# First cross-attention of a four-layer Flamingo stack: key weights folded into the query weights, value weights into the output weights

## The chip, the cores and the metric

The kernel runs on one core of one Trainium2 chip, in fp32. Its metric is the device time of one execution in microseconds (us). TensorE is written PE, VectorE DVE, ScalarE ACT, GpSimd POOL, and SyncE, which issues most loads, SP.

## The reference

Four layers, each a cross-attention and then a mixture of experts (or of LoRA adapters). x and the context are 16 batches of 128 tokens by 256 features. The change touches the attention of layer 0 only. It has 16 heads of 16 features, and each of the three projections is one 16x16 matrix that all heads share:

```python
kh = einsum('nshd,ed->nshe', k.reshape(N, S, 16, 16), Wk)     # k = ctx
qh = einsum('nshd,ed->nshe', q.reshape(N, S, 16, 16), Wq)     # q = layernorm(x)
vh = einsum('nshd,ed->nshe', v.reshape(N, S, 16, 16), Wv)     # v = ctx
attn = softmax(einsum('nqhd,nkhd->nhqk', qh, kh) / sqrt(16))
out = einsum('nhqk,nkhd->nqhd', attn, vh).reshape(N, S, 256) @ Wo.T
x = x + tanh(g_xattn[0]) * out
x = x + tanh(g_ffn[0]) * experts_0(layernorm(x))              # top 2 of 8, gelu
```

There is no bias in this attention, so energy = q Wq' Wk k' and out = attn v Wv' Wo' with block-diagonal matrices, and the products Wq' Wk and Wv' Wo' don't depend on the data.

## The kernel before

The 16 batches are handled in 4 blocks of 4 batches (512 tokens). A block is normalized (ln_block: statistics with bnst L250, xn on ACT L321, transposes ps_ln L344, xnT on ACT L348), projected to queries (ps_q L975) and keys (ps_k L975, copied to kT by ACT L1201). The queries are written twice, masked to even and odd heads (qM, one half by ACT L1225 and one by DVE L1220), so that one matmul of 32 rows serves two heads. Each batch then has its values projected (ps_v L987) and spread by an ACT copy (L1250) into one of three zeroed tiles in which each head has its own columns; its scores (ps_s L1259), exps (e, ACT L1274), values and denominators (ps_o L1315, 64 small matmuls), the reciprocal of the denominators (rs, DVE L1326), the product oT (DVE L1328), the output (ps_y L1337) and the addition to x (DVE L363). Each rs is also added to a running sum by POOL (sum_range L1126); rs has two buffers, so the reciprocal of batch b waits until POOL has added that of batch b-2.

Beside the attention runs what the experts need. POOL fills the sorted token buffer xg with zeros by 15 DMAs (L2416, function clear), from a tile made of a piece of kT. When a block of x is done, the router (front of Moe: ps_logitsT L426, ps_router L434, small DVE operations L377 to L553) finds the place of each token, and POOL scatters its rows into xg by 8 indirect DMAs (L558). After two blocks a plan of expert slots is made (DVE L637 to L722, its integers plan_i L712), SP reads it into registers and loads each slot's tokens (xr) and weights (w), and the first 12 slots of layer 0 (ps_h L1659, hT L1664, ps_e L866) are worked off, at first beside the rest of the routing.

The order of PE, ACT and DVE is written out by the kernel: the parts above are generators, a planner (class Clock) estimates from cost formulas when each part could start, and the part that is due is emitted. So a change in any part can change the whole order of the three engines. SP and POOL get their order from the framework's scheduler. DMAs of one queue are issued in its order.

```python
att = Fast16(0, pool, keys_in(pool), w, ctxT, watch)
attend([(att, clear, behind)], early(), eager=True, express=2)
```

Of the kernel before, what the change touches and what calls it, by code (L numbers as in the profile page):

```python
# [8 lines left out]
F32 = mybir.dt.float32  # L9
# [10 lines left out]
P = 128  # L20
B = 16
S = 128
D = 256
KC = D // P
NBLK = 4
BPB = B // NBLK
TB = BPB * S
H16, DH16 = 16, 16
# [62 lines left out]
def kernel(ctx: ExitStack, tc: tile.TileContext, a: dict, out: bass.AP):  # L91
    nc = tc.nc
# [6 lines left out]
    class Ring:  # L99


        def __init__(self, pool):
            self.pool, self.made = pool, []
# [8 lines left out]
    ps_x = Ring(ctx.enter_context(tc.tile_pool(name="ps_x", bufs=4, space=PSUM)))  # L112
# [6 lines left out]
    def load_x(bs):  # L119
# [7 lines left out]
    ident = const.tile([P, P], F32, tag="ident", name="ident")  # L127
# [3 lines left out]
        out=gates, in_=a["rows"][:, slice(*_ROWS["gates"])].to_broadcast([P, 8])  # L131
# [4 lines left out]
    def col(name, i):  # L136
        lo = _COLS[name][0] + i
        return cols[:, lo:lo + 1]

    def row(name):  # L140
        lo, hi = _ROWS[name]
        return rows[:, lo:hi]
# [14 lines left out]
    for e in range(NE):  # L157
# [9 lines left out]
        out=tri, in_=ones, compare_op=ALU.is_gt, fill=0.0, base=0,  # L167
# [27 lines left out]
    def tgx(i):  # L195
        return tg[:, i:i + 1]

    def gate_down(pool, i):

        gate = pool.tile([P, 1], F32, tag=f"gate{i}", name="gate", bufs=1)  # L200
        nc.vector.tensor_scalar(gate, tgx(i), DOWN, None, ALU.mult)
        return gate
# [780 lines left out]
    def project_values(layer, ps, w, src, tok):  # L983

        if layer == 0:
            for c in range(KC):
                nc.tensor.matmul(  # L987
                    ps[:, c * P:(c + 1) * P], lhsT=src[:, c, tok], rhs=w[:, 0, :],
                    start=True, stop=True,
                )  # L990
            return
        for k in range(KC):
            nc.tensor.matmul(
                ps, lhsT=src[:, k, tok], rhs=w[:, k, :], start=(k == 0), stop=(k == KC - 1)
            )
# [121 lines left out]
    class Watch:  # L1117
# [10 lines left out]
        def fine(self, good, behind):  # L1128
# [9 lines left out]
            nc.vector.tensor_reduce(good, eq, AX.X, ALU.add)  # L1138
            return self.n * P

    def keys_in(pool):
        return lambda: pool.tile([P, KC, TB], F32, tag="kT", name="kT", bufs=2)

    class Fast16:
# [3 lines left out]
        def __init__(  # L1148
            self, layer, pool, kpool, w, ctxT, watch, mask=None, bias=None, others=None
        ):  # L1150

            self.others = others
            self.bias = bias
            self.gate = tgx(1) if layer == 1 else gate_down(pool, layer)
            self.layer, self.pool, self.kpool = layer, pool, kpool
            self.ctxT, self.watch, self.mask = ctxT, watch, mask
            self.w = w

            self.qb = pool.tile([P, KC, 2], F32, tag=f"qb{layer}", name="qb", bufs=1)
            if layer == 0:  # L1160
                nc.vector.memset(self.qb, 0.0)
            else:
                for c in range(KC):
                    nc.vector.tensor_scalar(
                        self.qb[:, c, :], mask2, col(f"l{layer}_bq", c), None, ALU.mult
                    )

            self.vs = []
            for i in range(3):
                v = pool.tile([P, H16, 2 * DH16], F32, tag=f"v{layer}{i}", name="v", bufs=1)  # L1170
                nc.gpsimd.memset(v, 0.0)
                self.vs.append(v)
            self.qM, self.kT, self.es, self.os = {}, {}, {}, {}

        def prepare(self, blk, before):


            made = [self.queries(blk, before)]
            if blk not in self.kT:
                made.append(self.keys(blk))  # L1180
            if self.others is not None:

                if blk == 0:
                    made.append(self.keys(1))
                for later in (0, 1, 2) if blk == 0 else (3,) if blk == 1 else ():
                    made.append(self.others.keys(later))
            return made
# [43 lines left out]
        def scores(self, b, tick):  # L1231
            layer, pool = self.layer, self.pool
            wv = self.w[2]
            blk, tok = b // BPB, slice(b % BPB * S, (b % BPB + 1) * S)
            pv = ps_x.tile([P, H16, DH16], F32, tag="x", name="ps_v")
            project_values(layer, pv.rearrange("p h d -> p (h d)"), wv, self.ctxT[blk], tok)
            if layer == 1:
                v = pool.tile([P, H16, DH16], F32, tag="vb", name="vb", bufs=3)
            else:
                v = self.spread(self.vs[b % 3])  # L1240
                pv = pv.rearrange("p (j e) d -> p j e d", e=2)
            if layer:
                bv = row(f"l{layer}_bv")
                nc.vector.tensor_tensor(
                    v, pv,
                    bv.rearrange("p (h d) -> p h d", d=DH16) if layer == 1
                    else bv.rearrange("p (j e d) -> p j e d", e=2, d=DH16), ALU.add,
                )
            else:
                nc.scalar.copy(v, pv)  # L1250

            tick()


            pss = [ps_mm.tile([P, 4, S], F32, tag="mm", name="ps_s") for _ in range(4)]
            for c in range(KC):
                for j in range(4):
                    part = slice(j * 32, (j + 1) * 32)
                    nc.tensor.matmul(  # L1259
                        pss[j][:, 2 * c:2 * c + 2, :], lhsT=self.kT[blk][part, c, tok],  # L1260
                        rhs=self.qM[blk][part, c, :, tok], start=True, stop=True,
                    )
                if c == 0:
                    tick(False)
            es = []
            for j in range(4):
                e = pool.tile([P, 4, S], F32, tag="e", name="e", bufs=9)
                if layer == 2:
                    nc.scalar.activation(
                        e, pss[j], AF.Exp, bias=self.mask[0][:, b:b + 1],  # L1270
                        scale=self.mask[1][:, b:b + 1],
                    )
                else:
                    nc.scalar.activation(e, pss[j], AF.Exp)  # L1274
                es.append(e)
            self.es[b] = es
            if layer == 1:

                both = pool.tile([P, 2, H16], F32, tag="sums", name="sums")
                sums, rs = both[:, 0], both[:, 1]  # L1280
                by_pair = sums.rearrange("p (c j e) -> p j c e", c=KC, e=2)
                for j, e in enumerate(es):
                    nc.vector.tensor_reduce(
                        by_pair[:, j], e.rearrange("p (c e) s -> p c e s", e=2), AX.X, ALU.add
                    )
                nc.vector.reciprocal(rs, sums)
                self.watch.see(both.rearrange("p i h -> p (i h)"))
                nc.vector.tensor_tensor(
                    self.spread(self.vs[b % 3]), v.rearrange("p (j e) d -> p j e d", e=2),
                    rs.rearrange("p (j e) -> p j e", e=2)[:, :, :, None].to_broadcast(  # L1290
                        [P, H16 // 2, 2, DH16]
                    ), ALU.mult,
                )
            tick(False)
# [987 lines left out]
    watch = Watch(KC * S, "a")  # L2282
# [46 lines left out]
    def layers(fast):  # L2329
# [40 lines left out]
        with tc.tile_pool(name="context", bufs=1) as cpool, ExitStack() as for_mid:  # L2370
            ctxT = []
# [15 lines left out]
            with tc.tile_pool(name="att0", bufs=2) as pool:  # L2387
                w = attention_weights(0, pool)
# [57 lines left out]
                def early():  # L2446
                    while not started:
                        yield 1
                    yield from started[0]
# [5 lines left out]
                    lanes = []  # L2455
                behind, plans = routed(moe, turns, start)
                if fast:
                    att = Fast16(0, pool, keys_in(pool), w, ctxT, watch)
                    attend([(att, clear, behind)], early(), eager=True, express=2)
                else:  # L2460
                    general(shifted(pool, 0, w, ctxT), None, behind)
# [5 lines left out]
            with for_slots, tc.tile_pool(name="lanes0", bufs=2) as pool:  # L2467
                lanes = lanes + lane0(pool, LANES - len(lanes))
                job = slots0(moe, NSLOT - n, plans[-1:], lanes, tiles(fpool, bufs0))
                for i, _ in enumerate(job):  # L2470
                    if i == 24:
                        ws = [attention_weights(layer, wpool) for layer in (1, 2)]
                        if not biases:

                            t = stat.tile([P, BPB, ROW], F32, tag="xn", name="bias_rows", bufs=3)
                            nc.sync.dma_start(
                                out=t[:, 0, 0:D],
                                in_=a["l2_b2"][NE:NE + 1].to_broadcast([P, D]),
# [24 lines left out]
            with tc.tile_pool(name="mid", bufs=2) as pool:  # L2503
                lora = Lora(pool, wpool, biases["base_b"])
                if fast:
                    att = Fast16(
                        2, pool, lambda: shared_tile(spool, "kT"), ws[1], ctxT, watch, mask,
                        biases["l2_bo"],
                    )
# [29 lines left out]
        with ExitStack() as for_last:  # L2539
            with tc.tile_pool(name="ffn2", bufs=2) as pool:  # L2540
# [11 lines left out]
                if fast:  # L2552
                    wpool = right(for_last, "weights3")
                    att = Fast3(wpool, watch)
# [38 lines left out]
    ps = ps_x.tile([1, len(watches)], F32, tag="x", name="ps_good")  # L2593
# [9 lines left out]
    with tc.If(again > 0):  # L2603
        load_x(range(B))
        layers(fast=False)
# [90 lines left out]
```

## Time and profile before

| | |
|---|---|
| median of 8 runs | 1589.59 us (1586.75 to 1593.02) |
| profiled execution, its own time | 1587.12 us |
| span of its profile | 1585.4 us |
| mean granted PE clock | 0.977 |
| first attention with its routing | 0 to about 133 us |
| first 12 slots of experts | from 134.5 us |
| HBM read, written | 272.88 MB, 48.18 MB |

The span is the time between the first and the last instruction of the profile. Times inside the profile are counted from the start of the span. A line number L followed by digits is a line of the kernel before; in the changed kernel the lines behind the edits stand 21 to 42 further down (ps_s L1301, ps_o L1357, rs L1368, oT L1370, ps_y L1379, the v copy L1288, the zero fills L2458).

### The profile page before, as it was taken

The numbers are of one execution on the slowest core, as the hardware profiler recorded it, in microseconds if no ns is written. First come the engines' busy times: TensorE is split into PE (matmuls) and PEld (weight loads), VectorE is DVE, ScalarE is ACT, GpSimd is POOL, SyncE is SP. The second block draws the span as 40 slices with busy tenths as digits, with TensorE's granted clock in tenths as the row PEclk, the third lists the DMA queues.
The fourth block names the chain that finished last, engine by engine and source line by source line (L and its number), as shares of the span: only waits on it lengthen the run. The fifth ranks groups of instructions, "written<-read, shape, count | busy, mean of one in ns | idle before, by whom it ended". The sixth has DMA issues, their size and how long they took to land.

```text
span 1585.4 us, 34879 instructions
## 1 busy us (share of the span) xinstructions
PE 1483.1 (94%) x12752; PEld 1171.9 (74%) x12752; DVE 864.6 (55%) x2763; ACT 649.0 (41%) x1550; POOL 369.0 (23%) x485
## 2 busy tenths in 40 slices
PE   6897899999999999899999999999999999997992
PEld 4676889999656567655559999999955656677892
DVE  3685312222279767766346555556743627477655
ACT  5566323335556566652125333334453334224110
POOL 4242411111532212434000110111150002023531
PEclk9899999999999999999999999999999999999996
DMA  9914683534420000111064412411351000033956
GB/s 322 384 41 152 193 267 99 198 98 148 98 40 1 2 6 23 43 41 54 0 238 148 154 48 99 165 32 32 105 109 19 14 1 29 2 102 124 312 171 215
DMA packets 109368, 171.52 MB, mean 108 GB/s; under 512 B 17273, under 2 KB 79294, under 8 KB 109184
## 3 DMA queue, kind: packets, MB, share of 16 engines
q1 hardware_dynamic: 85344, 114.22, 22.6%
q0 software_dynamic: 20304, 49.66, 10.0%
q10 hardware_dynamic: 3536, 5.25, 1.0%
q8 instruction: 108, 1.77, 0.4%
q14 instruction: 76, 0.62, 0.1%
HBM read 272.88 MB, written 48.18 MB: 203 GB/s over the span
## 4 chain that ended last, share of the span: by engine, by line
PE 79%; DVE 10%; DMA 5%; ACT 3%; issue 2%; POOL 0%; SPq 0%; DVEq 0%; ACTq 0%; POOLq 0%
PE ps_w L1836 16%; PE ps_e L866 12%; PE ps_h L1659 7%; PE ps_w L1773 7%; PE ps_qk L2096 5%; PE ps_v L2205 3%; PE ps_o L1315 3%; PE ps_s L2226 2%; PE ps_q L978 2%; PE ps_g L1884 2%; PE ps_y L2274 2%; PE ps_y L1337 2%; PE ps_s L1794 2%; PE ps_s L1259 2%; PE ps_k L978 2%
## 5 line engine op out<-in xcount | busy, mean ns | idle before, releaser
L1836 PEld LDWEIGHTS ps_w<-xT,w 128*128 128x128 f32 x2304 | 264.3, 192 | 2.5 <-issue 0.2
L1836 PE MATMUL ps_w<-xT,w 128*128 128x128 f32 x2304 | 265.1, 275 | 0.0
L878 POOL DMA_INDIRECT yd<-y,to x117 | 118.6, 1014 | 569.9 <-DVE c L841 305.8
L866 PE MATMUL ps_e<-w,hT 128*128 128x256 f32 x848 | 197.8, 380 | 2.5 <-DVE hT L1743 1.9
L866 PEld LDWEIGHTS ps_e<-w,hT 128*128 128x128 f32 x848 | 154.8, 190 | 21.4 <-DVE hT L1743 2.8
L1844 ACT ACTIVATE u<-ps_w,b 128x128 f32<-128x128 f32 x312 | 89.5, 367 | 175.4 <-PE ps_w L1836 170.3
L1659 PE MATMUL ps_h<-xT,w 128*128 128x128 f32 x1120 | 137.4, 283 | 13.8 <-DMA w<-in_l_w_dram 7.0
L1659 PEld LDWEIGHTS ps_h<-xT,w 128*128 128x128 f32 x1120 | 135.7, 199 | 16.8 <-issue 8.6
L1847 DVE SCALAR_TENSOR_TENSOR m<-ps_w,b,u 128x128 f32<-128x128 f32 x312 | 87.6, 344 | 109.0 <-PE ps_w L1836 94.8
L1664 ACT ACTIVATE hT<-ps_h,b 128x128 f32<-128x128 f32 x312 | 88.6, 373 | 129.4 <-issue 82.5
L558 POOL DMA_INDIRECT xg<-xn,xi x96 | 93.7, 976 | 99.2 <-issue 53.0
L1773 PE MATMUL ps_w<-xnT,sw 128*128 128x512 f32 x256 | 111.9, 594 | 0.0
L874 DVE SCALAR_TENSOR_TENSOR y<-ps_e,c,bias 128x256 f32<-128x256 f32 x78 | 37.6, 483 | 135.1 <-PE ps_e L866 134.3
L1126 POOL TENSOR_TENSOR sum_range<-sum_range,rs 128x256 f32<-128x256 f32 x48 | 35.3, 736 | 247.5 <-DVE rs L2253 137.7
L1773 PEld LDWEIGHTS ps_w<-xnT,sw 128*128 128x128 f32 x256 | 48.3, 190 | 56.7 <-issue 50.9
L831 DVE COPY xT<-ps_xr 128x256 f32<-128x256 f32 x117 | 48.6, 418 | 75.4 <-PE ps_xr L829 75.4
L1326 DVE RECIPROCAL rs<-ps_o 128x256 f32<-128x256 f32 x32 | 56.1, 1754 | 32.9 <-PE ps_o L1315 22.9
L1274 ACT ACTIVATE e<-ps_s 128x512 f32<-128x512 f32 x128 | 65.9, 602 | 18.5 <-PE ps_s L1259 18.5
L321 ACT ACTIVATE xn<-x,nmr,rstd 128x256 f32<-128x256 f32 x128 | 67.8, 596 | 12.4 <-DVE nmr L314 9.1
L2232 ACT ACTIVATE e<-ps_s 128x512 f32<-128x512 f32 x64 | 33.5, 601 | 74.3 <-PE ps_s L2226 74.2
L1315 PE MATMUL ps_o<-e,v 128*32 128x128 f32 x1536 | 53.5, 282 | 9.2 <-DVE x L363 3.9
L858 ACT ACTIVATE bias<-b,c 128x256 f32<-128x256 f32 x78 | 40.5, 519 | 51.6 <-DVE c L844 20.8
(272 smaller groups left out, 2550.5 us busy)
## 6 DMA issues: line engine op xcount, KB each, us to landing
w<-in_l_w_dram SPq DMA_DIRECT2D x160, 1024.0 KB
w<-in_l_w_dram SPq DMA_DIRECT2D x39, 512.0 KB
kT<-in_l_wgu_dram SPq DMA_DIRECT2D x39, 512.0 KB
xg<-zeros POOLq DMA_DIRECT2D x15, 1170.0 KB, 25.3
b<-in_l_b_dram SPq DMA_DIRECT2D x80, 128.0 KB
xr<-xg SPq DMA_DIRECT2D x78, 130.0 KB
kT<-in_l_w_dram SPq DMA_DIRECT2D x39, 256.0 KB
x<-yd POOLq DMA_DIRECT2D x48, 128.0 KB, 4.6
```

What stands on the lines that cost most here:

```text
L321: nc.scalar.activation(xns[:, i, 0:D], src, AF.Identity, bias=nmr[:, i:i + 1], scale=rstd[:, i:i + 1])
L558: self.unordered(nc.gpsimd.indirect_dma_start(out=xg[:, :], in_=xns[:, i, :], in_offset=None, out_offset=bass.IndirectOffsetOnAxis(ap=xi[: ...
L866: nc.tensor.matmul(po, lhsT=hT[:, f, :], rhs=lane(s)["w2"][:, f, :], start=(f == 0), stop=(f == nf - 1),)
L878: self.unordered(nc.gpsimd.indirect_dma_start(out=yd[:, :], in_=y, in_offset=None, out_offset=bass.IndirectOffsetOnAxis(ap=to[:, 0:1], axi ...
L1315: nc.tensor.matmul(po[32 * j:32 * (j + 1), i, c, :], lhsT=w if i else v[:, c * HPC + 2 * j + e, :], rhs=es[j][:, 2 * c + e, :], start=(e = ...
L1659: nc.tensor.matmul(ps[:, i, :], lhsT=w["w1"][:, k, f * P:(f + 1) * P], rhs=xT[:, k, :], start=(k == 0), stop=(k == KC - 1),)
L1664: nc.scalar.activation(hT[:, f, :], ps[:, i, :], AF.Gelu, bias=w["b1"][:, f:f + 1])
L1773: nc.tensor.matmul(ps, lhsT=wt[:, k, f * P:(f + 1) * P], rhs=xnT[:, k, :], start=(k == 0), stop=(k == KC - 1),)
L1836: nc.tensor.matmul(ps[:, f, :], lhsT=wt[:, k, s, f * P:(f + 1) * P], rhs=xT[:, k, :], start=(k == 0), stop=(k == KC - 1),)
L1844: nc.scalar.activation(u[:, f, :], pair[0][:, f, :], AF.Identity, bias=w["b1"][:, i:i + 1])
L1847: nc.vector.scalar_tensor_tensor(m1[:, f, :], pair[1][:, f, :], w["b3"][:, i:i + 1], u[:, f, :], ALU.add, ALU.mult,)
L2096: nc.tensor.matmul(ps, lhsT=w[:, k, c * P:(c + 1) * P], rhs=src[:, k, :], start=(k == 0), stop=(k == KC - 1),)
```

## The change

At the start PE turns Wq, Wk and Wv (each laid out as a 128x128 block-diagonal of its 16x16 matrix), and makes two products from them: Wq' Wk, which takes the place of Wq, and Wv' Wo', which takes the place of Wo. Then the keys are the context itself, which is already in SBUF transposed (ctxT), and the values are the context itself in rows. Projections of keys and values with their copies are gone. The rows of the context are loaded by SP, 512 KB for each block, that of block blk+1 when block blk is prepared; the tile has two buffers. ACT spreads them where it spread the projected values. The zeros for xg are made from ctxT instead of kT. Since the planner sees other parts, it writes another order for the three engines up to the first slots.

```diff
+    def folded(pool, w):
+        wq, wk, wv, wo = w
+        ps = ps_x.tile([P, 3, P], F32, tag="x", name="ps_turned")
+        for i, v in enumerate((wq, wk, wv)):
+            nc.tensor.transpose(ps[:, i, :], v[:, 0, :], ident)
+        t = pool.tile([P, 3, P], F32, tag="turned", name="w_turned", bufs=1)
+        nc.vector.tensor_copy(t, ps)
+        ps = ps_x.tile([P, P], F32, tag="x", name="ps_qk0")
+        nc.tensor.matmul(ps, lhsT=t[:, 0, :], rhs=t[:, 1, :], start=True, stop=True)
+        both = pool.tile([P, 1, P], F32, tag="wqk", name="w_qk", bufs=1)
+        nc.vector.tensor_copy(both[:, 0, :], ps)
+        ps = ps_x.tile([P, KC, D], F32, tag="x", name="ps_vo0")
+        for c in range(KC):
+            nc.tensor.matmul(
+                ps[:, c, :], lhsT=t[:, 2, :], rhs=wo[:, c, :], start=True, stop=True
+            )
+        out = pool.tile([P, KC, D], F32, tag="wvo", name="w_vo", bufs=1)
+        nc.vector.tensor_copy(out, ps)
+        return [both, None, None, out]
...
+            self.rows = {}
+            if layer == 0:
+                self.kT = dict(enumerate(ctxT))
+                self.load_rows(0)
+
+        def load_rows(self, blk):
+            t = self.pool.tile([P, BPB, D], F32, tag="crows", name="ctx_rows")
+            nc.sync.dma_start(
+                out=t,
+                in_=a["ctx"][blk * TB:(blk + 1) * TB, :].rearrange("(b p) d -> p b d", p=P),
+            )
+            self.rows[blk] = t
...
         def prepare(self, blk, before):
+            if self.layer == 0 and blk + 1 < NBLK:
+                self.load_rows(blk + 1)
             made = [self.queries(blk, before)]
             if blk not in self.kT:
                 made.append(self.keys(blk))
...
-            pv = ps_x.tile([P, H16, DH16], F32, tag="x", name="ps_v")
-            project_values(layer, pv.rearrange("p h d -> p (h d)"), wv, self.ctxT[blk], tok)
+            if layer:
+                pv = ps_x.tile([P, H16, DH16], F32, tag="x", name="ps_v")
+                project_values(
+                    layer, pv.rearrange("p h d -> p (h d)"), wv, self.ctxT[blk], tok
+                )
...
-                nc.scalar.copy(v, pv)
+                nc.scalar.copy(
+                    v, self.rows[blk][:, b % BPB, :].rearrange(
+                        "p (j e d) -> p j e d", e=2, d=DH16
+                    )
+                )
...
-                    att = Fast16(0, pool, keys_in(pool), w, ctxT, watch)
+                    att = Fast16(0, pool, None, folded(pool, w), ctxT, watch)
```

More of the change, by code (lines that the diff above doesn't have):

```diff
@@ L1240, in scores @@
                 v = self.spread(self.vs[b % 3])
-                pv = pv.rearrange("p (j e) d -> p j e d", e=2)
             if layer:
@@ L1244, in scores @@
                 nc.vector.tensor_tensor(
-                    v, pv,
+                    v, pv if layer == 1 else pv.rearrange("p (j e) d -> p j e d", e=2),
                     bv.rearrange("p (h d) -> p h d", d=DH16) if layer == 1
```

## The prediction

> **What bounds the kernel now.** I read the page's engine totals first, then the stage table over the first attention, then the waits of VectorE (DVE) and GpSimd (POOL), the chain of waits, and POOL's timeline. The totals say TensorE (PE); the stage table corrects that for the only stretch that the change touches.
>
> ```profile
> PE 1483.1 (94%) x12752; PEld 1171.9 (74%) x12752; DVE 864.6 (55%) x2763; ACT 649.0 (41%) x1550; POOL 369.0 (23%) x485
> ```
> ```profile
> 0.00:50.00 50.00, 35.64 (x400) 22.15 (x400) 17.82 (x49) 27.79 (x54) 21.88 (x71) 0.93 0.96 336
> 50.00:100.00 50.00, 47.10 (x674) 34.72 (x678) 38.98 (x111) 32.11 (x72) 12.97 (x17) 0.90 0.65 244
> 100.00:133.00 33.00, 27.00 (x493) 20.65 (x482) 30.16 (x88) 15.63 (x35) 14.15 (x20) 1.00 0.17 56
> 133.00:240.00 107.00, 92.99 (x607) 86.79 (x608) 32.24 (x163) 45.51 (x122) 25.42 (x28) 0.94 0.67 216
> ```
> Columns: stretch, length, busy us of PE, weight loads, DVE, ACT, POOL, then PE clock, DMA share, GB/s. PE is full only in 50 to 100 us (47.1 of 50). Before that it idles 14.4 us while the DMA engines are saturated (0.96); after it DVE is the full engine (30.2 of 33); from 133 to 240 PE idles 14 us at the start of the expert slots, and later it is full to the end. So PE work that goes pays at face value in one stage of three.
>
> What ends the first stage is a queue on POOL:
>
> ```profile
> DVE rs L1326 <- POOL sum_range L1126: 7.4, 1, 7.4
> POOL xg L2416 <- DMA xg<-zeros: 16.5, 6, 3.5
> ```
> ```profile
> 23.05 22.97 DMA xg<-zeros
> ...
> 46.92 0.88 POOL sum_range L1126
> ...
> 47.82 1.77 DVE rs L1326
> ```
> The first pair reads: waiting engine and line, releaser, total us, times, longest. POOL issues fifteen zero fills of 1170 KB; nine go out at once and each of the last six waits for a landing. Behind them stands POOL's first sum_range, which frees the two-buffer tile rs. So the third reciprocal (batch 2) waits 7.4 us on DVE until 47.82. That is gate 1. Gate 2 is of the same kind:
>
> ```profile
> 89.70 1.11 POOL L558 DMA_INDIRECT xg<-xn,xi  x1 [5.23 <-ACT xn L321]
> ...
> 98.71 0.96 POOL L558 DMA_INDIRECT xg<-xn,xi  x1 [0.30 <-issue]
> 99.70 0.74 POOL L1126 TENSOR_TENSOR sum_range<-sum_range,rs 128x256 f32<-128x256 f32 x1
> ```
> The eight scatters of a routed block hold POOL for about 10 us (89.70 to 99.67) ahead of a sum_range; the reciprocal of batch 10 follows at 100.63.
>
> **What goes and comes.** Key projection: 16 matmuls, 10.62 us of PE, and eight kT copies, 4.68 us of ACT. Value projection: 64 matmuls, 11.29 us of PE. Together 21.9 us of PE; by stage 11.7 before 50 us, 7.6 in 50 to 100, 2.6 in 100 to 133. Fold: three transposes (0.29 us, row of ps_ln), one 128x128 product (0.30, row of ps_v) and two of 256 columns (0.41, row of ps_y) make 2.0 us; by the cold ps_k rows at the start (1.1 us against 0.6 later) up to 3.7. It lies where PE has 3.75 us of work (now removed) before 14.95 us; if that cover failed, 2 to 4 us would fall on the first block, ahead of gate 1, which swallows them. Its three DVE copies, about 1.3 us, stand ahead of the first LayerNorm's small operations, in DVE's 3.06 us wait for ACT: nothing.
>
> The sixteen v copies stay on ACT, now reading SBUF. No row shows this copy; ACT's copy from PSUM is 375 ns on average (347 the shortest), its 128x256 operation from SBUF, xn, 596 ns. So 0 to +3.5 us of ACT in all; a saving can't be excluded (265 ns for the half-size logitsT gives -1.8). I take +1.5: the shape is that of the first, the memory that of the second, and 4.7 us of kT copies go besides. ACT is never full here (15.6 of 33, 32.1 of 50), and the 1.15 us of ps_s hide a copy. Once v was late by more than that, each exp behind it on ACT would be late by the rest.
>
> [...]
>
> **What moves, and this decides.** (1) The context comes a second time, as rows: four loads of 512 KB. The first two go out on SP's queue behind the last x loads, at about 20.2 and 20.7 us by the rows of the loads issued there now; that is after POOL's first nine fills. The 1.05 MB go through saturated engines (387 GB/s in a typical slice of that stretch): 2.7 us. A third load wants its buffer when block 0's values are copied; some 0.8 us more of it fall ahead of the last fill. Bounds: 0 (rows served behind the fills) to 4.1 (a third load in full). I take +3.5, so the reciprocal of batch 2 starts at 51.3 for 47.82. The first v copy (25.85 now) waits for its rows until some 30 to 33 us, because a 128 KB load of that queue took 0.9 to 1.5 us; ACT's exp of batch 0 (26.11 now) is queued behind it, and PE behind that. Gate 1 covers this: three batches at about 4 us of PE fit before 51.
>
> (2) The planner writes another order. DVE's two masked query writes of block 1 (1.52 us) stand ahead of the reciprocal of batch 2 now (at 37.86), and behind it and its oT after the change. So the scores of batch 4 wait for gate, reciprocal 1.77, oT 0.43 and qM 0.8 to 1.5: about 54.5, against 52.83. Block 3's qM likewise goes behind the reciprocal of batch 10, which gate 2 holds.
>
> (3) Between 51 and 90 PE does 7.6 us less, and this wins back some of the 3.5. But DVE has 39 us of work in that stage plus the moved 1.5 and becomes the full engine; the block's routing needs its last x through the same DVE. My walk along the new orders with the durations above gives, now and after: reciprocal of batch 7 at 81.8 and 83.5, of batch 8 at 88.7 and 90.5; scatter from 89.7 and about 90.5; batch 10, behind the scatter, 100.6 and 101.6; batch 12, 114.6 and 115.2. Here the loss is almost regained.
>
> (4) The second block's scatter moves. Now it stands ahead of the sums of batches 12 and 13 and ends at 123.7. After, its positions are written just ahead of the reciprocal of batch 13 (121.6), and the sum of batch 13 is behind it: 121.6 + 8 x 1.26 + 0.8 = 132.5. The reciprocal of batch 15 waits for that buffer: 132.8, against 128.7 now. The last x add starts a reciprocal (1.77), an oT (0.43) and an output (1.3, from 130.89 to 132.17) later: 136.3 for 132.17.
>
> (5) The plan's integers (plan_i L712, 122.72 now, 9 us ahead of the last x) come behind the last x and small operations of the routing on DVE, at about 139.3. SP's plan reads and weight loads follow them; now it takes SP 11.7 us from the plan to the issue of slot 1's first weights (122.96 to 134.66) and some 5 us to land. Two loads of the next attention's weights are placed ahead of the plan read on SP, and wait for the last work of this attention, so they add little. Slot 1's first products start at 156 to 158 instead of 143.50. Against that, front work that PE does there now (two LayerNorm transposes, the router: 2.6 us) and slot 0's second half are done in the wait. Slot 1's second half starts at 166.8 to 168.8, against 160.60: +6 to +8. The later weight stall (4.3 us at 183.6) shrinks by 0 to 2, as the scatters no longer share the queue. From 240 us the PE order is the same in both kernels and PE is full, so what is left arrives at the end: +4 to +8, and I take +5, in the lower half because the walk adds every wait at full length.
>
> [...]
>
> **The sum.** The profiled execution took 1587.12 us (span 1585.4, 1.7 around it), 2.5 below the median 1589.59. With +5: 1592.1 for such an execution, 1594.5 for the median.
>
> **Rivals.** *A gain.* If the rows are served behind the fills, gate 1 stays at 47.8; the 7.6 us of PE in 50 to 100 then count for about 5 (DVE binds for the rest), the last x comes at 127 to 129, and the plan's later place costs nothing that PE hasn't won: 1582 to 1586. For it: PE's 47.1 of 50; against it: both gates and the full DVE of 100 to 133. *Nothing.* Gate 1 at +2, some 4 us won, and slot 1 late by 2 to 4: 1588 to 1592. *A larger loss.* One mechanism, at SP: the next layer's weight loads ahead of the plan read hold it until the last exp and sum_range, and the 11.7 us chain starts after that; slot 1's second half slips by 10 to 13 us: 1599 to 1603. It decides as soon as the read is later than 142 us. *The fold does not do what it says*: the products and copies named above are gone from the changed order, so I give this nothing.
>
> **The numbers.** What a measurement of this kernel can tell from no change is about 0.2%, 3.2 us. Forecast (1592.5 to 1598) 0.50; gain 0.15; nothing 0.18; larger loss 0.17. Of the forecast 0.05 lies within 3.2 us: faster 0.15, same 0.23, slower 0.62. The range 1585.5 to 1602 leaves out most of the gain (0.12) and the end of the loss (0.07).
>
> **What would show it.** Right: the first sum_range at 50 to 51 instead of 46.92; a DVE wait on POOL at batches 2, 10 and 15; the last x add at 135 to 139; slot 1's first products past 154; then an equal shift to the end. Wrong: a first sum_range by 48, or a last x add before 132, which would mean that PE's saving got through; or a shift that goes away again between 170 and 240 us in weight stalls that the slots have anyway.

## The result, and the profile after

On chips where the kernel before takes 1589 us the changed kernel is slower: median 1602.15 us (16 runs) against 1589.12 (45 runs of the kernel before), ratio 1.0081, 95% interval 1.0071 to 1.0092, about +13 us. The forecast had the side and the places right and the size too small (+5): the median lies 0.15 us above the upper end of its range (1602). A later comparison on another chip, where the kernel before takes 1664 us, gave 0.9979 (0.9964 to 0.9993) for the same pair; the last section returns to it. Everything up to there is from chips of the first kind unless it says otherwise.

The profiled execution of the changed kernel took 1600.13 us (span 1598.3). Engine totals, then the stage table with the columns of the prediction (stretch, length, busy us of PE, weight loads, DVE, ACT, POOL, PE clock, DMA share, GB/s):

```profile
PE 1479.3 (93%) x12681; PEld 1168.6 (73%) x12681; DVE 864.7 (54%) x2766; ACT 639.9 (40%) x1538; POOL 369.0 (23%) x485
```
```profile
0.00:50.00 50.00, 29.05 (x297) 18.92 (x297) 16.93 (x47) 22.48 (x44) 19.57 (x69) 0.86 0.96 334
50.00:100.00 50.00, 43.60 (x727) 31.61 (x727) 40.88 (x112) 32.48 (x74) 14.37 (x20) 0.93 0.76 285
100.00:133.00 33.00, 26.26 (x441) 20.42 (x441) 24.28 (x68) 15.72 (x35) 11.33 (x14) 0.84 0.10 34
133.00:240.00 107.00, 88.21 (x549) 79.90 (x550) 35.90 (x173) 37.47 (x107) 28.27 (x33) 0.87 0.65 207
```
PE is busier in no stage than before, and its granted clock is lower in three of the four: 0.86 for 0.93 before 50 us, 0.84 for 1.00 in 100 to 133, 0.87 for 0.94 behind it. The profile's windows show where: the clock is 0.50 from 52 to 58 us, from 104 to 108 and from 138 to 156. PE is called cold there, and warm where the clock is 1.00. DVE, 91% busy in 100 to 133 before, now waits there too (24.3 of 33). The waits of DVE and POOL name the gates (waiter, releaser, total us, times, longest):

```profile
DVE rs L1368 <- POOL sum_range L1126: 13.9, 3, 6.6
```
```profile
POOL xg L2458 <- DMA xg<-zeros: 19.0, 7, 4.6
```
Three reciprocals wait for POOL instead of one: batch 2 (6.60 us), batch 10 (4.42) and batch 15 (2.90). How PE comes out of the first of these is seen in its timeline (start, length, line, what, and in brackets the idle time before it with its releaser):

```profile
53.10 2.09 PE L1301 MATMUL ps_s<-qM,ctxT 32*128 32x256 f32 x16 [5.32 <-DVE qM L1256]
55.12 1.94 PE L1357 MATMUL ps_o<-e,v 128*32 128x128 f32 x32
...
59.54 1.15 PE L1301 MATMUL ps_s<-qM,ctxT 32*128 32x256 f32 x16
60.61 1.08 PE L1357 MATMUL ps_o<-e,v 128*32 128x128 f32 x32
```
The scores wait 5.32 us for block 1's qM, and then the same sixteen matmuls take 2.09 us that take 1.15 a batch later. The last of the three waits, batch 15, stands behind the second block's scatter and one sum (POOL, then DVE):

```profile
133.47 0.96 POOL L558 DMA_INDIRECT xg<-xn,xi  x1 [0.30 <-issue]
134.46 0.73 POOL L1126 TENSOR_TENSOR sum_range<-sum_range,rs 128x256 f32<-128x256 f32 x1
```
```profile
135.22 1.76 DVE L1368 RECIPROCAL rs<-ps_o 128x256 f32<-128x256 f32 x1 [2.90 <-POOL sum_range L1126]
```
The end of the attention and the start of the slots, on DVE and on PE:

```profile
139.67 0.48 DVE L363 SCALAR_TENSOR_TENSOR x<-ps_y,gate,x 128x256 f32<-128x256 f32 x1
...
141.19 0.18 DVE L712 CAST plan_i<-plan 128x36 int32<-128x36 f32 x1
```
```profile
137.58 2.05 PE L1379 MATMUL ps_y<-w_vo,oT 128*128 128x256 f32 x4 [5.16 <-DVE oT L1370]
...
147.91 3.42 PE L418 MATMUL ps_router<-wgl,xnT 128*128 128x8 f32 x16
...
152.40 6.10 PE L1701 MATMUL ps_h<-xT,w 128*128 128x128 f32 x32 [0.55 <-DVE xT L831]
...
159.24 3.84 PE L1701 MATMUL ps_h<-xT,w 128*128 128x128 f32 x32 [0.30 <-DVE xT L831]
...
169.62 5.47 PE L1701 MATMUL ps_h<-xT,w 128*128 128x128 f32 x32 [2.47 <-DMA w<-in_l_w_dram]
```
The last x add is 7.5 us late (132.17 before), the plan 18.5. Behind them PE works cold: router 3.42 us (1.85 before), slot 0's first products 6.10 (3.84 when warm), and PE waits 2.47 us for slot 2's weights. The kernel before has a cold place here too, one slot later: slot 1's first products take 6.62 us behind a wait of 4.73.

### The profile page after: what moved, and what is told of

Same layout as the page of the kernel before. It is cut to its first block, busy times and chain, and to the rows that moved or that the text cites. A ratio compares the mean times of both kernels' runs of the same rounds, so it can differ in the third digit from the quotient of the medians.

```text
span 1598.3 us, 34723 instructions
## 1 busy us (share of the span) xinstructions
PE 1479.3 (93%) x12681; PEld 1168.6 (73%) x12681; DVE 864.7 (54%) x2766; ACT 639.9 (40%) x1538; POOL 369.0 (23%) x485
## 4 chain that ended last, share of the span: by engine, by line
## 5 line engine op out<-in xcount | busy, mean ns | idle before, releaser
L1368 DVE RECIPROCAL rs<-ps_o 128x256 f32<-128x256 f32 x32 | 56.2, 1756 | 43.6 <-PE ps_o L1357 26.7
```

The lines of the kernel that those rows point to most:

```text
L1368: nc.vector.reciprocal(rs, po[:, 1])
```

## Experiments

The first four ran on one chip with the kernel before at 1591.14 us. The changed kernel was not run beside them; its loss is taken from the first comparison. The table takes the places of their profiles; "same matmul" is one ps_e of the slots behind which all orders agree.

| us in the profile | before | changed | no_rows | pad_order | before_no_sum | no_sum |
|---|---|---|---|---|---|---|
| reciprocal, batch 2 | 47.82 | 50.11 | 47.55 | 54.48 | 41.81 | 42.21 |
| reciprocal, batch 10 | 100.63 | 101.59 | 99.19 | 104.71 | 97.56 | 87.03 |
| reciprocal, batch 15 | 128.69 | 135.22 | 132.95 | 132.79 | 124.10 | 116.25 |
| plan_i | 122.72 | 141.19 | 138.91 | 126.81 | 119.48 | 122.00 |
| last x add | 132.17 | 139.67 | 137.39 | 137.22 | 127.57 | 120.50 |
| slot 0, second half | 150.57 | 163.53 | 161.33 | 155.04 | 144.81 | 143.38 |
| same matmul | 242.47 | 253.88 | 249.25 | 246.61 | 236.19 | 232.92 |
| span | 1585.4 | 1598.3 | 1590.8 | 1592.3 | 1582.9 | 1580.8 |

**The order of the kernel before (pad_order).** The planner is charged for projections that are not there:

```diff
+        def charge(self, n, columns):
+            t = ps_x.tile([P, n * columns], F32, tag="x", name="ps_none")
+            each = 2 * max(columns / 1200, 0.107)
...
+            self.at[PE] += n * each
...
             else:
+                none = clocks[-1].charge(KC, S)
...
                 nc.scalar.copy(
```


> The changed kernel, but the planner is charged for the key and value projections as if they were still there, so that PE, ACT and DVE get the written order of the kernel before, less the removed instructions (rows of the context are still loaded, weights still folded). Theory (the loss comes from the new written order: block 1's and block 3's masked queries behind a gated reciprocal, the second scatter ahead of one sum more, the plan behind the last x): at least 8 of the 13 us come back, 1586 to 1594. Rival (the second load of the context costs the time, through the fills and the late first rows): 1599 or more. Rival (PE, with less work, idles and its clock falls, whatever the order): 1598 or more.

Measured: 1591.81 us, 1.0007 (0.9982 to 1.0032) of the kernel before. So with the old order the loss is gone (expected: 1586 to 1594), though fold, copies and rows are all there. The step from the last x add to slot 0's second half is 17.8 us, against 23.9 in the changed order (18.4 before): the plan's place is worth about 6 us. The saving of PE does not show either, and ACT's timeline says why:

```profile
37.16 0.41 ACT L1297 COPY v<-ctx_rows 128x256 f32<-128x256 f32 x1 [11.21 <-DMA ctx_rows<-in_ctx_dram]
```
The first rows landed at 37.16 in this execution (28.62 in that of the changed kernel), so late that batch 2's reciprocal came at 54.48, with PE and not POOL as its releaser: a new wait in the old one's place.

**No rows (no_rows).**

```diff
-                    v, self.rows[blk][:, b % BPB, :].rearrange(
+                    v, xs[b].rearrange(
```


> The changed kernel with its written order kept instruction for instruction, but without the four loads of context rows: the value copies read the batch of x that lies in SBUF (this changes the values, so the attention's result is another one). Theory of the order: only the shift of the first sum_range (49.22 against 46.92) and the wait for the first rows go, 2 to 4 us, 1598 to 1600. Rival of the second load: all of the loss goes, 1587 to 1591.

Measured: 1592.89 us, 1.0018 (0.9996 to 1.0039). More than the theory allowed (1598 to 1600). On the path to the last x add the rows cost what was expected, 2.3 us. The rest comes later. From slot 0's second half to slot 1's it is 11.6 us in the changed kernel (163.53 to 175.14) and 7.2 here (161.33 to 168.57). The third block's scatter starts at 149.86 in the changed kernel and slot weights go out at 150.25, behind it; here they go out at 147.56, ahead of the scatter's 147.58, and PE has no weight wait at that place. The lines, of the changed kernel and then of no_rows:

```profile
149.86 1.06 POOL L558 DMA_INDIRECT xg<-xn,xi  x1 [9.36 <-DVE xi L555]
150.25 1.39 SPq L1653 DMA_DIRECT2D w<-in_l_w_dram  x2
```
```profile
147.56 0.43 SPq L1650 DMA_DIRECT2D w<-in_l_w_dram  x2
147.58 1.06 POOL L558 DMA_INDIRECT xg<-xn,xi  x1 [9.36 <-DVE xi L555]
164.78 3.73 PE L1698 MATMUL ps_h<-xT,w 128*128 128x128 f32 x32
```
no_sum, below, agrees: weights at 131.64 behind a scatter at 130.65, and a wait of 3.16 us. I read this from three profiles; no kernel moved it alone. So a good part of what no_rows gains may hang on which of two transfers goes out first, and not on the rows' bytes.

**No running sums (no_sum, before_no_sum).**

```diff
-                self.watch.see(rs.rearrange("p c s -> p (c s)"))
+                if self.layer:
+                    self.watch.see(rs.rearrange("p c s -> p (c s)"))
```


> The changed kernel with its written order kept on PE, ACT and DVE, but without POOL's running sums over the reciprocals of the first attention (a range guard is left out), so no reciprocal waits for POOL. The 13.9 us of DVE waits for POOL go. Theory (gates times written order): reciprocals of batches 2, 10 and 15 start by up to 6, 4 and 3 us earlier, the last x add at 130 to 134 instead of 139.7, the plan with it: 1592 to 1597. Rival of the second load or of the removed cover alone: 1600 or more.

> The kernel before without the same sums of the first attention. PE idled only 2.0 us at the first gate and 1.7 to 2 us at two later ones, and DVE is full from 100 us on: 2 to 5 us faster than before, 1584 to 1587. If the gates cost the kernel before as much as the changed one, 1580 or less.

Measured: no_sum 1583.09 us, 0.9967 (0.9945 to 0.9988); before_no_sum 1585.62, 0.9987 (0.9963 to 1.0011). The second came as expected; the first went further than expected (1592 to 1597, the last x add at 130 to 134). With the order and the rows of the change kept, taking POOL out of the reciprocals brings the last x add forward by 19.2 us (139.67 to 120.50), in the kernel before by 4.6 (132.17 to 127.57). The changed kernel is then 7.1 us ahead of before_no_sum at that point, close to the 7.6 us of PE work that went from 50 to 100 us. It gives 5.6 of them back by slot 0's second half (22.9 us from the last x add, against 17.2), behind the late plan. Its stage from 50 to 100 us shows a full and warm PE:

```profile
50.00:100.00 50.00, 46.68 (x834) 33.76 (x828) 41.83 (x118) 36.62 (x83) 9.33 (x12) 1.00 0.75 285
```
834 matmul records against 727 in the changed kernel, 46.7 us busy against 43.6, at a clock of 1.00 against 0.93.

**Fills on SP (fills_sp, pad_fills_sp, before_fills_sp) and early rows (rows_early).** These ran on a chip where the kernel before takes 1664.22 us; only ratios on it are read.

```diff
-                            nc.gpsimd.dma_start(
+                            nc.sync.dma_start(
                                 out=xg[i:i + n * P, :].rearrange(
```
```diff
-            nc.sync.dma_start(
+            (nc.sync if blk else nc.scalar).dma_start(
                 out=t,
                 in_=a["ctx"][blk * TB:(blk + 1) * TB, :]...
```


> The changed kernel, same written order on PE, ACT and DVE, the fifteen zero fills issued by SP instead of POOL; so the first sum_range stands behind no fill (gate 1 goes), while the scatters stay on POOL (gates 2 and 4 stay). The 6.6 us wait of batch 2's reciprocal goes; the later two (4.4 and 2.9) stay or grow. Theory (gate 1 is the largest part): 1587 to 1593. If gate 1 only hides behind gate 2 and the second scatter: 1598 or more, with the last x add again near 139.

> The order of the kernel before (planner charged for the projections), weights folded, rows loaded, and the fills on SP. Both parts of the loss go, so PE's saving in 50 to 100 us should show: 1579 to 1586, faster than the kernel before by 3 to 10. If the late first rows (batch 0 cannot start before its rows) bound this order: 1588 or more.

> The kernel before with the fills on SP. It waited 7.4 us on DVE but only 2.0 us on PE at gate 1: 1585 to 1588. Equal to the kernel before within 2 us if its later stages give that back.

> The changed kernel, same order on PE, the first block's rows loaded on ACT's queue behind the transposed context, ahead of the fills and of the last x loads. Theory (the first rows' lateness is covered by gate 1, only their bytes ahead of the fills count): 1 to 2 us better at most, 1600 to 1602, batch 0's reciprocal at 31 to 33 instead of 36.75 and batch 2's still near 49 to 50. If the late first copy is what costs: 1595 or less.

Measured, as ratios to the kernel before: fills_sp 0.9898 (0.9869 to 0.9927), pad_fills_sp 0.9901 (0.9877 to 0.9925), before_fills_sp 0.9996 (0.9978 to 1.0014), rows_early 0.9972 (0.9949 to 0.9994). Without the fills ahead of the sums, batch 2's reciprocal starts at 40.87 in fills_sp. Batch 10's still waits 7.9 us for POOL's scatter, the gate that the edit left. Both kernels with the fold came out better than expected (1587 to 1593 and 1579 to 1586, which is 0.999 to 1.002 and 0.994 to 0.998 of 1589). The kernel before gains nothing from the same edit. rows_early has batch 0's reciprocal at 32.25 and batch 2's at 50.38, as the theory had it: gate 1 covers the late rows.

**Beside the changed kernel.** The last four runs, on such a chip (before: 1664.30 us), are the changed kernel itself, the key fold alone, the changed kernel with the fills on SP, and the one with all three causes undone.

> The changed kernel itself, beside the next three on their chip, so that each can be set against it and against the kernel before. 1.0071 to 1.0092 of the kernel before, as its first comparison gave; if the loss hangs on this chip's transfers, it moves by more than 0.3%.

> Only the key weights are folded: values are projected as before, no rows are loaded, and the written order stays that of the kernel before as far as block 2, with the plan ahead of the last x. PE loses 10.6 us of work, 8.4 of it ahead of gate 1. Theory (rows and order make the loss): the same as before or up to 3 us faster, 0.998 to 1.001 of it. Rival (less PE work by itself makes PE cold and slow): 1.003 or more.

> The changed kernel with the fifteen fills on SP, again beside the others: on the slower chip it was 0.9869 to 0.9927 of the kernel before. Theory (gate 1 is what made the loss): at least 8 us better than the changed kernel on this chip, 0.990 to 1.001 of the kernel before.

> All three causes undone: the order of the kernel before, fills on SP, the first block's rows on ACT's queue ahead of the fills. Batch 0's reciprocal at 30 to 33, no wait for POOL at batch 2; PE's saving of 7.6 us in 50 to 100 should show as far as DVE lets it: 0.990 to 0.997 of the kernel before, the best of all. If DVE binds from 50 us on: within 2 us of the fills_sp version.

Measured: changed_beside 1660.78 us, 0.9979 (0.9964 to 0.9993); keys_only 1664.59, 0.9994 (0.9978 to 1.0010); fills_sp_beside 1650.87, 0.9908 (0.9892 to 0.9924); pad_fills_early 1651.35, 0.9916 (0.9894 to 0.9938). The first is a plain miss. The two with the fills on SP are 9 to 10 us better than the changed kernel beside them; fills_sp leaves nothing of the computation out and is faster than both kernels there. It was not run on a chip of the first kind. pad_fills_early is in its expected range but no better than fills_sp: on these chips the old order adds nothing once the fills have left POOL. Folding the keys alone neither gains nor loses; but the whole change does not lose there either, so this says little on whether less PE work is itself the harm. Against that speaks pad_order on the first kind of chip: the same PE work is gone, and the loss with it.

## Why the prediction was right, and where it fell short

*Gate 1* was put 3.5 us later; it came 2.3 later (first sum_range 49.22 for 46.92, reciprocal 50.11 for 51.3 forecast). *The masked queries behind the gate* came as forecast: scores of batch 4 at 53.10 for 54.5. *Batches 7, 8 and 10* were put at 83.5, 90.5 and 101.6 and came at 82.97, 89.85 and 101.59. *The second scatter ahead of the sum of batch 13* held batch 15's reciprocal until 135.22; the forecast was 132.8. *The plan behind the last x* came at 141.19 for 139.3. The experiments bear out the three causes: take away the gates, the order or the rows, and at least three quarters of the 13 us are gone by the medians. They do not add up; as I read the traces they act in series: rows push the gate, the order puts block 1's and block 3's queries behind it, and the late plan passes the delay on to the slots. All of this is from chips of the first kind.

What was mis-sized is, first, the duration of PE's work behind a wait, in steps (3) and (4). The walk used warm rows there. The changed kernel's waits leave PE idle for 5.32 (gate 1), 4.46 (gate 2) and 5.16 us (the last reciprocal), and the clock in 100 to 150 us is 0.76 where it was 0.93. Batch 10 came on the forecast; batch 12, forecast at 115.2, came at 117.22, behind eight ps_ln of 1.94 us that take 1.09 warm and ps_s of 2.09 for 1.15. With ps_y at 2.05 for 1.03 the last x add is 3.4 us later than forecast (139.67 for 136.3).

Second, a wait that step (5) put at nothing. From the last x add to slot 1's first products it had 19.7 to 21.7 us, and 19.57 were measured, so the cold router and slot 0's cold products cost nothing beyond the forecast. From there to slot 1's second half it had 10.8 us, and 15.90 were measured (159.24 to 175.14): 2.47 us of them are PE's wait for slot 2's weights, 1.74 the cold products behind it (5.47 for 3.73). Together this is +14.7 at slot 1's second half where the sum had +6 to +8. Later weight stalls gave back 3.3 (forecast 0 to 2): +11.4 at the same matmul, and 1.5 more come behind it. The queue that the forecast has scatters and weight loads share is not in the profile of the kernel before: the eight scatters from 89 to 100 us moved 0.93 MB in queue q0, SP's four weight loads from 52 to 88 us 4.19 MB in q1. No run kept PE warm by itself, so the share of the cold clock is read from the rows and not shown by an experiment.

One term was counted wrong without harm: the fold's products. Each product of the fold appears as two matmuls in the profile (ps_qk x2 for one, ps_vo x4 for two), and the 2.0 us took one for each; PE was busy with the fold for 3.58 us (0.87, 0.80 and 1.91), within the 3.7 of the cold bound and ahead of gate 1.

Behind the three waits above (4.46 to 5.32 us) the granted clock is 0.50, and the rows are 1.8 to 2 times as long (ps_ln 1.94 us for 1.09, ps_s 2.09 for 1.15, ps_y 2.05 for 1.03). A shorter wait has the same behind it: PE waits 1.96 us before 125.91, the clock is 0.50 from 126.5 to 129.5, and ps_o takes 1.94 us for 1.08. Behind one of 1.85 us, before 195.09, the clock stays at 1.00 and ps_h takes 3.81 us for 3.73. What decides between the two was not tried.

Of the rivals, the larger loss named the right size (1599 to 1603) with the wrong mechanism. SP read the plan 0.2 us after the write of plan_i began, and the next layer's weight loads had gone out 0.5 to 0.9 us before it, so they held nothing. Of the v copies, the medians are 398 ns from SBUF (changed kernel) and 372 from PSUM (kernel before), +26 ns each. The taken +1.5 us was too much (0.4 in all).

## What to carry to other kernels

Before work is taken off the busiest engine, find what releases each stage: here a guard sum on POOL queued behind DMA issues, so that of the 21.9 us of PE work that went nothing came off the time: PE waited instead (5.32, 4.46 and 5.16 us at the three places), and worked at a granted clock of 0.50 behind the waits. Where a planner writes the order from estimated costs, compare the two orders and look for work that now stands behind a wait its model doesn't know. A 2x2 of change and gate (19.2 us against 4.6) says more than either alone.

## What the runs showed of the hardware

The same pair of kernels differs in sign by chip: 1.0081 on the first kind, 0.9979 on the other. On the slower chips PE's timeline has gaps without a releaser, as here beside POOL's scatters (92.67 to 102.65 us in this profile of the changed kernel):

```profile
96.60 1.34 PE L1357 MATMUL ps_o<-e,v 128*32 128x128 f32 x31
98.43 0.27 PE L1357 MATMUL ps_o<-e,v 128*32 128x128 f32 x1 [0.49 <-issue]
98.44 0.29 PE L1357 MATMUL ps_o<-e,ones 128*32 128x128 f32 x1
99.82 0.31 PE L1357 MATMUL ps_o<-e,ones 128*32 128x128 f32 x2 [1.09 <-issue]
100.55 0.27 PE L1357 MATMUL ps_o<-e,ones 128*32 128x128 f32 x1 [0.41 <-issue]
101.26 0.66 PE L1357 MATMUL ps_o<-e,ones 128*32 128x128 f32 x4 [0.44 <-issue]
```
PE gets a few instructions, then nothing for 0.4 to 1.1 us (0.41 to 1.09 in these lines). Over the whole span such waits are 31 to 37 us in the eight profiles from these chips, against 0.7 in each of the two profiles that open this document; the clock over the whole span is 0.951 to 0.963, against 0.969 and 0.977 in those two. These gaps do not explain the sign: they are 36.8 us in the changed kernel, 34.1 in keys_only and 31.1 in before_fills_sp, which has all the PE work of the kernel before. There is no profile of the kernel before on such a chip; keys_only is the nearest, with its time (0.9994) and most of its order. At the same matmul of the slots it is at 261.71 us and the changed kernel at 263.73; on the first kind the kernel before is at 242.47 and the changed one at 253.88. So up to there keys_only is some 19 us behind the kernel before on the first kind, the changed kernel only 10 behind itself, and most of the loss is gone by that place. This compares one profile of each, 4 us below and above their medians. Why it is so, and why PE is starved, was not tried: both stay open.
